# A factorization layer in a bilinear seven-product scheme: the first group begins with P1, and its sums T1 and T2 are made by VectorE

## The chip, the cores and the metric

The kernel runs on one core of a Trainium2 chip. The metric is device time in microseconds of one execution. The kernel before takes 1285.91 us, the median of three runs (1285.85 to 1286.28). Lower is better.

## What is computed

For a batch `x` (1024 x 512), a weight tensor (64 x 512 x 512), and a linear layer:

```python
out_lin = x @ lin_w.T + lin_b
xv = einsum('bf,efm->bem', x, weight)
zp = einsum('bf,efm->bem', square(x), square(weight))
interaction = 0.5 * sum(square(xv) - zp, axis=1)
return out_lin + interaction
```

The sum of `zp` over e is one product of `square(x)` with the weights' squares summed over e, so nearly all of the work is `xv`: a product of 1024 x 512 with 512 x 32768, of which each element is squared and added up over e.

## The kernel before

**Tiles and stages.** `xv` is made in 32 groups of 1024 columns each (loop over `h` at L773). In a group the product is split into 2 x 2 quadrants on each side: `x` into A11, A12, A21, A22 and the group's weights into w11, w12, w21, w22. Instead of eight products of quadrants there are seven, P1 to P7, of sums of quadrants (`OPERAND` names the sum on the side of x, `RHS` the weights'): P1 = A11 x w11, P2 = A12 x w21, P3 = R3 x w22, P4 = A22 x T4, P5 = R5 x T1, P6 = R6 x T2, P7 = R7 x (w12 + w22); signs stand on the side of x. T1 is the sum of the quadrants 0 and 1 (w11, w12), T2 is T1 plus quadrant 3 (w22), T4 is T2 plus quadrant 2 (w21); they are successive states of one tile T. The sums on the side of x (R5, R6, R7, R3) are made once.

**Three passes or plain.** A product of fp32 numbers is made of fast fp32r matmuls in three passes: both sides are split into pieces H, L and K, and H x H, L x L and K x K are added up with weights. A split (`split`, L627) of a weight tile takes ScalarE two passes (L, then H), GpSimd or VectorE one for L (by `SPLIT`, and by `FIRST` in group 0), and GpSimd one for K. In group 0 the products in `PLAIN` (P1 and P2) take the quadrants as they are, with plain fp32 matmuls: eight of 128 x 128 x 512, each recorded as two. A product in three passes has 24 short ones. Every product has two halves, each in a bank pair of PSUM (four pairs in turn), and the K pass of a product comes `LAG` half-halves after its H and L passes, behind the front of the next product. Between the two passes the bank is scaled or added to by VectorE (L366) or ScalarE.

**What goes from product to product.** P1's banks are copied to two tiles `p1`, P5's to tiles `p5` (L741, ScalarE); P6 adds p1 and p5 and keeps the sum in tiles `w`; P2, P3, P7 and P4 add p1 or w, and their results are squared by ScalarE (`sq`) and reduced by VectorE (`acc`). The squares of the weights (`wsq`) are made by ScalarE and reduced by VectorE for `zp`.

**Order of the products.** Within a group `ORDER` is P1, P6, P2, P3, P7, P5, P4, where the P5 is that of the next group. Group 0's own P5 stands ahead of the loop (L772).

**Before group 0** the linear layer is computed with the same scheme one level deep, in plain fp32 (L504, seven products of sixteen records each), while the quadrants of x are loaded and split (`x_pieces`, L482). Its four results lie in tiles that group 0 uses later: L12 in `p5_0`, L22 in `p1_0`, L21 in `p1_1`, L11 in `wsq_0`. They are added up by VectorE and stored to a buffer in DRAM (`lind`) by SP; only after the store may the tile be used again.

**Loads.** SP loads quadrants of weights (L606). The sums T and P7's operand are made by DMAs that add to a tile as they land (`dma_add` in `load_more`, L611), issued by GpSimd. The L and K pieces of A12 and A22 (`X2L`, `X2K`, `X4L`, `X4K`) are also made by such accumulate DMAs.

**What sets the order.** Nothing of it is written out by hand. Every operation is added to a list with its cost, reads and writes (`Plan.add`); a planner (`Plan.forward`) then gives every engine's queue its order by due times that follow from TensorE's fixed sequence, in 60 rounds with random changes of due times, and the best is kept. Each engine then runs its queue in order. A changed operation can therefore move others in the whole program. Operations of VectorE marked `both` read two tiles in SBUF; the planner puts them where GpSimd has no instruction that reads SBUF, or orders the two. In the first 70 us a DMA can be tied to the matmul that ended last before its planned start (`mark`).

**The tail.** After group 31 the products for `zp` are made like the linear layer; what `acc` holds is turned, stored to DRAM (`accd`), and added to the linear part in the tiles p1 and p5 by accumulate DMAs.

Of the kernel before, what the change touches and what calls it, by code (L numbers as in the profile page):

```python
# [22 lines left out]

PE, DVE, ACT, POOL, SP = "PE", "DVE", "ACT", "POOL", "SP"

PLAIN = (1, 2)
LAG = 4
ORDER = (1, 6, 2, 3, 7, 5, 4)
SPLIT = {**dict.fromkeys(range(1, 8), POOL), 2: DVE, 3: DVE}
MORE = True  # L30
X_SPLIT = {5: DVE, 6: DVE, 3: DVE, 7: DVE, 1: DVE, 2: "DMA", 4: "DMA"}
FIRST = dict.fromkeys(range(1, 8), POOL)
SCALE = {1: "DVE", 5: "ACT"}
RAW = {"w11": 2, "w12": 2, "w21": 1, "w22": 2, "T": 2}
PIECES = {"H": 3, "L": 3, "K": 3}
# [6 lines left out]
class Plan:  # L42
# [104 lines left out]
    def forward(self, chain):  # L147
# [4 lines left out]
        running = dict.fromkeys(pending)  # L152
        times = [self.HOP]
        done, late, nxt, wire, held, mark = [], 0.0, 0, [12.0], None, None
# [55 lines left out]
        while len(done) < len(ops):  # L210
            now = heapq.heappop(times)
            moved = True
            while moved:
                moved = False
                for e in pending:
                    if free[e] > now + 1e-6:
                        continue
                    o = pick(e, now)
                    if e == POOL and held is not None and (o is None or o.move):
                        ends(DVE, held, now + held.costs[DVE])  # L220
                        held = None
                    if o is None:
                        continue
                    moved = True
                    if e == PE:
                        nxt, mark = nxt + 1, running[PE]
                        late = max(late, now - o.latest)
                    cost = o.costs[e]
                    o.start, o.engine = now, e
                    if o.move and o.emit and mark and now < self.EARLY[0] and now > max(  # L230
                        ready(o, e) + 0.3, free[e] + 0.1
                    ):
                        o.after = mark
                    tensor = e == POOL and not o.move
                    if e == DVE and o.both and free[POOL] > now + 0.05 and not running[POOL].move:
                        held, free[e], o.end = o, float("inf"), float("inf")
                    elif tensor and held is not None and held.latest < o.latest + self.YIELD:
                        ends(DVE, held, now + held.costs[DVE])
                        o.after, held = held, None
                        ends(e, o, free[DVE] + 0.15 + cost)  # L240
                    elif tensor and held is None and free[DVE] > now and running[DVE].both:
                        o.after = running[DVE]
                        ends(e, o, free[DVE] + cost)
                    else:
                        ends(e, o, now + cost)
                    for f in o.costs:
                        pending[f].discard(o.n)
                    done.append((o, e))
                    for x in o.succ:
                        left[x] -= 1  # L250
                        if not left[x]:
                            release(ops[x])
# [4 lines left out]
def kernel(  # L257
# [47 lines left out]
    buf = {}  # L305
# [21 lines left out]
    raw = {q: ring(q, n, block) for q, n in RAW.items()}  # L327
# [42 lines left out]
    def dve(o, a, b, sub, reads, writes, size=512, both=False):  # L370
        def emit(_):
            return (nc.vector.tensor_sub if sub else nc.vector.tensor_add)(o, a, b)  # L372

        plan.add({DVE: 0.06 + 1.08 * size / 1024}, emit, reads, writes, both=both)

    def pool(o, a, b, sub, reads, writes, size=1024):
        def emit(_):
            return (nc.gpsimd.tensor_sub if sub else nc.gpsimd.tensor_add)(o, a, b)  # L378

        plan.add({POOL: 0.1 + 2.24 * size / 1024}, emit, reads, writes)  # L380
# [14 lines left out]
    def dma_add(o, i, reads, writes, move=3.1, land=2.5):  # L395
        plan.add(
            {POOL: 0.62}, lambda _: nc.gpsimd.dma_start(o, i, accum_op=ALU.add),  # L397
            tuple(reads) + tuple(writes), writes, land=land, move=move,
        )
# [200 lines left out]
    QUAD = ("w11", "w12", "w21", "w22")  # L600
    RHS = {1: "w11", 2: "w21", 3: "w22", 4: "T", 5: "T", 6: "T", 7: "w12"}
    now = {}

    def src(h, q):
        return weight[h // NCB, q][:, h % NCB]

    def load(h, n, q):
        now[h, n] = raw[n]()
        dma(buf[now[h, n]], src(h, q), (), (now[h, n],))

    def load_more(h, n, q):  # L611

        o = now[h, n]
        if h or MORE:
            dma_add(buf[o], src(h, q), (), (o,))
        else:
            i = now[h, QUAD[q]]
            pool(buf[o], buf[o], buf[i], False, (o, i), (o,))

    def w_squares(h, q):  # L620
        row, col = divmod(QUAD.index(q), 2)
        n, sq = now[h, q], wsquare()
        act(buf[sq], buf[n], AF.Square, (n,), (sq,))
        m = (h // NCB) * MG + (2 * col + h % NCB) * MI
        reduce(w2_sum[:, ts(row, KH), m:m + MI], buf[sq], (sq,), (("w2", row, m),))
# [16 lines left out]

    def prepare(h, p):
        if p == 5:
            load(h, "T", 0)
            if h:
                load_more(h, "T", 1)
                load(h, "w11", 0)
            load(h, "w12", 1)
            if not h:  # L650
                load_more(h, "T", 1)
                load(h, "w11", 0)
                load(h, "w22", 3)
                load(h, "w21", 2)
            w_squares(h, "w12")
        if p == 1:
            if h:
                load(h, "w22", 3)
            w_squares(h, "w11")
        if p == 6:  # L660
            load_more(h, "T", 3)
            if h:
                load(h, "w21", 2)
            w_squares(h, "w22")
        if p == 2:
            w_squares(h, "w21")
        if p == 7:
            load_more(h, "w12", 3)
        if p == 4:
            load_more(h, "T", 2)  # L670
        n = now[h, RHS[p]]
        return n if not h and p in PLAIN else split(n, SPLIT[p] if h else FIRST[p])

# [15 lines left out]
    def product(h, p):  # L689
        ops, plain = prepare(h, p), not h and p in PLAIN  # L690
        for half in range(2):
# [77 lines left out]

    for g in range(NG):  # L770
        acc_name[g] = acc_ring()
    product(0, 5)  # L772
    for h in range(NH):  # L773
        for p in ORDER:
            if p != 5:
                product(h, p)
            elif h + 1 < NH:
                product(h + 1, p)
            if not h:
                give_back(*(n for n in ("A11", "A12", "A22") if OPERAND[p] == n))  # L780
        if h % NCB == NCB - 1 and h + 1 < NH:
            turn(h // NCB)
# [64 lines left out]
    for (r, c), n in (((0, 0), "p1"), ((1, 0), "p1"), ((1, 1), "p5"), ((0, 1), "p5")):  # L847
        n = o_name[r, c] = kept[n]()
# [45 lines left out]
    for r in (1, 0):  # L894
        dma(buf[last][:, r], acc_dram[:, M // P - 1, ts(r, H)], acc_names(M // P - 1),
            ((last, r),), 1.0)
        n = o_name[r, 1]
# [56 lines left out]
```

## Time and profile before

| | |
|---|---|
| median of three runs | 1285.91 us |
| lowest, highest | 1285.85, 1286.28 us |
| the profiled execution | 1285.96 us, of which 1284.0 from the first instruction to the last |
| granted TensorE clock | 0.999 of full speed |
| moved by DMA | 171.93 MB, 134 GB/s over the span |

Instructions are named by engine: PE is TensorE's matmul and PEld its weight load, DVE is VectorE, ACT ScalarE, POOL GpSimd, SP SyncE. A row of a timeline has the start in us from the span's start, the duration, the engine, the line, the operation, what is written from what (numbers of buffers left out), the size, how many follow each other, and in brackets the idle time ahead of it with what ended it. Matmuls are pipelined and their ends are modelled, so the durations of neighbours overlap; times between starts are safer. In rows of DMAs stand the size of each and the median time from issue to landing. Names of pieces and tiles are cut in some rows: the tiles of the weights' quadrants and the kept tiles `w` both read `w`.

### The profile page before, as it was taken

How to read it: one execution, taken by the hardware profiler on the slowest of the kernel's cores; microseconds unless marked ns; L12 is line 12 of the kernel's file. 1: busy time of each engine (PE TensorE's matmuls, PEld its weight loads, DVE VectorE, ACT ScalarE, POOL GpSimd, SP SyncE). 2: the span in 40 equal slices, each digit the busy share in tenths (PEclk: the TensorE clock that was granted, in tenths of full speed). 3: DMA queues.
4: the chain of work that ended last, by engine and by line, in shares of the span. 5: the costliest groups of instructions: out<-in, count | busy, mean ns of one | idle time of the engine just before them, and what ended most of it. 6: DMA issues, size and time to landing. Idle time of an engine off the chain costs nothing.

```text
span 1284.0 us, 15422 instructions
## 1 busy us (share of the span) xinstructions
PE 1277.9 (100%) x5476; PEld 1024.1 (80%) x5476; DVE 1224.3 (95%) x1018; ACT 963.9 (75%) x1005; POOL 1043.5 (81%) x532
## 2 busy tenths in 40 slices
PE   9999999999999999999999999999999999999998
PEld 4688888888888888888888888888888888888883
DVE  7799999999999999999999999999999999999996
ACT  6677877777787777877777878777778777787781
POOL 2888898888898888898888888888889878889881
PEclk9999999999999999999999999999999999999999
DMA  8966654446654445664445664444665435665456
GB/s 237 210 175 148 148 118 123 101 108 151 148 129 123 99 110 139 152 142 118 108 102 130 148 152 115 120 98 114 152 148 128 120 85 122 145 152 131 126 112 168
DMA packets 68077, 171.93 MB, mean 134 GB/s; under 512 B 22944, under 2 KB 23968, under 8 KB 68000
## 3 DMA queue, kind: packets, MB, share of 16 engines
q0 software_dynamic: 20448, 72.89, 33.4%
q1 hardware_dynamic: 45296, 94.91, 22.1%
q10 hardware_dynamic: 2256, 3.15, 0.7%
q8 instruction: 43, 0.70, 0.2%
q14 instruction: 34, 0.28, 0.1%
HBM read 160.43 MB, written 6.29 MB: 130 GB/s over the span
## 4 chain that ended last, share of the span: by engine, by line
PE 94%; DVE 3%; DMA 2%; ACT 0%; issue 0%; ACTq 0%; SPq 0%; DVEq 0%
PE bank L697 92%; PE bank L522 2%; DMA w<-weight 1%; DMA p<-lin_wT 1%; DVE pL L366 0%; DVE bank L366 0%; DVE acc L385 0%; DVE X3K L366 0%; DVE p L372 0%; DVE w L372 0%; ACT pH L360 0%; ACT sq L360 0%; ACTq L427 0%; DVE X7K L366 0%; DVE sq L366 0%
## 5 line engine op out<-in xcount | busy, mean ns | idle before, releaser
L378 POOL TENSOR_TENSOR pK<-pH,pL 128x1024 fp32r<-128x1024 f32 x222 | 570.8, 2574 | 161.9 <-PE bank L697 157.5
L360 ACT ACTIVATE sq<-bank 128x1024 f32<-128x1024 f32 x256 | 261.9, 1024 | 93.8 <-issue 48.5
L385 DVE TENSOR_REDUCE acc<-sq 128x16 f32<-128x1024 f32 x256 | 308.5, 1205 | 1.3 <-ACT sq L360 1.2
L378 POOL TENSOR_TENSOR pL<-T,pL 128x1024 fp32r<-128x1024 f32 x96 | 256.7, 2674 | 12.9 <-ACT pH L360 10.7
L366 DVE SCALAR_TENSOR_TENSOR bank<-bank,w 128x1024 f32<-128x1024 f32 x192 | 233.8, 1218 | 0.7 <-PE bank L697 0.6
L372 DVE TENSOR_TENSOR w<-bank,p 128x1024 f32<-128x1024 f32 x128 | 155.6, 1216 | 26.8 <-PE bank L697 26.7
L360 ACT ACTIVATE p<-bank 128x1024 f32<-128x1024 f32 x128 | 131.0, 1023 | 59.9 <-PE bank L697 59.4
L366 DVE SCALAR_TENSOR_TENSOR pL<-pH,w 128x1024 fp32r<-128x1024 f32 x62 | 167.4, 2700 | 0.0
L366 DVE SCALAR_TENSOR_TENSOR bank<-bank,p 128x1024 f32<-128x1024 f32 x128 | 153.0, 1216 | 5.4 <-ACT p L360 4.5
L360 ACT ACTIVATE pL<-T 128x1024 fp32r<-128x1024 f32 x96 | 101.1, 1054 | 75.5 <-issue 68.3
L385 DVE TENSOR_REDUCE w_sum<-wsq 128x16 f32<-128x1024 f32 x128 | 154.1, 1204 | 2.5 <-ACT wsq L360 2.5
L378 POOL TENSOR_TENSOR pL<-w,pL 128x1024 fp32r<-128x1024 f32 x64 | 154.4, 2412 | 0.4 <-issue 0.4
L360 ACT ACTIVATE pH<-w 128x1024 fp32r<-128x1024 f32 x126 | 133.0, 1056 | 11.9 <-PE bank L697 10.3
L360 ACT ACTIVATE wsq<-w 128x1024 f32<-128x1024 f32 x128 | 134.6, 1052 | 0.4 <-DVE w_sum L385 0.4
L397 POOL DMA_DIRECT2D T<-weight x96 | 92.5, 963 | 36.7 <-POOL pL L378 17.5
L360 ACT ACTIVATE pH<-T 128x1024 fp32r<-128x1024 f32 x96 | 101.2, 1054 | 0.0
L360 ACT ACTIVATE pL<-w 128x1024 fp32r<-128x1024 f32 x64 | 67.9, 1061 | 43.6 <-PE bank L697 25.0
L697 PE MATMUL bank<-pH,X4H 128*128 128x512 f32 x256 | 81.4, 399 | 0.0
L697 PE MATMUL bank<-pH,X6H 128*128 128x512 f32 x256 | 78.9, 389 | 0.3 <-ACT p L360 0.3
L697 PE MATMUL bank<-pH,X5H 128*128 128x512 f32 x256 | 79.2, 391 | 0.0
L697 PE MATMUL bank<-pL,X4L 128*128 128x512 f32 x256 | 79.1, 390 | 0.0
L697 PE MATMUL bank<-pH,X3H 128*128 128x512 f32 x256 | 78.9, 390 | 0.1
(114 smaller groups left out, 2545.8 us busy)
## 6 DMA issues: line engine op xcount, KB each, us to landing
w<-weight SPq DMA_DIRECT2D x128, 512.0 KB, 5.8
T<-weight POOLq DMA_DIRECT2D x96, 512.0 KB, 6.1
T<-weight SPq DMA_DIRECT2D x32, 512.0 KB, 4.8
w<-weight POOLq DMA_DIRECT2D x32, 512.0 KB, 6.8
accd<-turned SPq DMA_DIRECT2D x64, 32.0 KB, 5.8
p<-lind SPq DMA_DIRECT2D x4, 512.0 KB, 4.5
out<-p ACTq DMA_DIRECT2D x8, 256.0 KB, 2.5
w<-xT SPq DMA_DIRECT2D x6, 256.0 KB, 4.9
```

Of the source, the lines that this page charges most:

```text
L360: nc.scalar.activation(o, i, func, bias=bias, scale=scale)
L366: return nc.vector.scalar_tensor_tensor(o, i, scalar, j, ALU.mult, op)
L372: return (nc.vector.tensor_sub if sub else nc.vector.tensor_add)(o, a, b)
L378: return (nc.gpsimd.tensor_sub if sub else nc.gpsimd.tensor_add)(o, a, b)
L385: lambda _: nc.vector.tensor_reduce(o, i.rearrange("p a (m e) -> p a m e", e=E), axis=AX.X, op=ALU.add),
L397: {POOL: 0.62}, lambda _: nc.gpsimd.dma_start(o, i, accum_op=ALU.add),
L522: made = nc.tensor.matmul(buf[bank[u]], b[:, k, ts(u, P)], a[:, k, :], start=first and k == 0, stop=k == KH - 1, skip_group_check=True,)
L697: made = nc.tensor.matmul(buf[bank, j], buf[x][:, k, ts(2 * half + j, P)], buf[w][:, k, :], start=first and k == 0, stop=k == KH - 1, skip ...
```

## The change

Group 0 is reordered and its operands are made in another way; the later groups' operations are the same.

- P1 of group 0 comes first, then its P5, then P6, P2, P3, P7, the next group's P5, and P4. Before, its P5 came first and P1 second.
- All four quadrants of group 0 are loaded as they are, w11, w12, w22, w21. T1 = w11 + w12 and T2 = T1 + w22 are VectorE additions into two tiles of the ring T (`sum_of`), instead of a load and two accumulate DMAs into one. T4 is still an accumulate DMA, into T2's tile.
- T1's L piece is made by VectorE (`FIRST`), not GpSimd.
- P2 of group 0 is made in three passes, and so w21 is split, and A12's pieces are needed there.
- The planner's `mark` skips an entry that has no instruction, and `MORE`, which was always true, is gone.

```diff
-PLAIN = (1, 2)
+PLAIN = (1,)
-MORE = True
-FIRST = dict.fromkeys(range(1, 8), POOL)
+FIRST = {**dict.fromkeys(range(1, 8), POOL), 5: DVE}
...
-                        nxt, mark = nxt + 1, running[PE]
+                        nxt += 1
+                        if running[PE] and running[PE].emit:
+                            mark = running[PE]
...
         o = now[h, n]
-        if h or MORE:
-            dma_add(buf[o], src(h, q), (), (o,))
-        else:
-            i = now[h, QUAD[q]]
-            pool(buf[o], buf[o], buf[i], False, (o, i), (o,))
+        dma_add(buf[o], src(h, q), (), (o,))
+
+    def sum_of(n, a, b):
+
+        o, a, b = raw[n](), now[0, a], now[0, b]
+        now[0, n] = o
+        dve(buf[o], buf[a], buf[b], False, (a, b), (o,), 1024, True)
...
         if p == 5:
-            load(h, "T", 0)
             if h:
+                load(h, "T", 0)
                 load_more(h, "T", 1)
                 load(h, "w11", 0)
-            load(h, "w12", 1)
-            if not h:
-                load_more(h, "T", 1)
-                load(h, "w11", 0)
-                load(h, "w22", 3)
-                load(h, "w21", 2)
+                load(h, "w12", 1)
+            else:
+                sum_of("T", "w11", "w12")
             w_squares(h, "w12")
         if p == 1:
             if h:
                 load(h, "w22", 3)
+            else:
+                for q in (0, 1, 3, 2):
+                    load(h, QUAD[q], q)
             w_squares(h, "w11")
         if p == 6:
-            load_more(h, "T", 3)
             if h:
+                load_more(h, "T", 3)
                 load(h, "w21", 2)
+            else:
+                sum_of("T", "T", "w22")
             w_squares(h, "w22")
...
-    product(0, 5)
     for h in range(NH):
         for p in ORDER:
             if p != 5:
                 product(h, p)
             elif h + 1 < NH:
                 product(h + 1, p)
+            if not h and p == 1:
+                product(h, 5)
```

How it moves instructions. In the names below the first number is the buffer in its ring: `w11_0` is quadrant w11 of group 0, while `w11_1` and `w12_1` hold A11 and A12 at this time.

TensorE, the first products behind the linear part, before:

```order
L522 MATMUL bank_3_117<-w_0_109,p5_2_113 128x512 x4
L697 MATMUL bank_0_114<-pH_0_95,X5H_77 128x512 x2
L697 MATMUL bank_0_114<-pL_0_98,X5L_78 128x512 x2
...
L697 MATMUL bank_2_116<-w11_0_86,w11_1_87 128x512 x4
L697 MATMUL bank_0_114<-pK_0_101,X5K_79 128x512 x4
L697 MATMUL bank_3_117<-w11_0_86,w11_1_87 128x512 x4
L697 MATMUL bank_1_115<-pK_0_101,X5K_79 128x512 x4
L697 MATMUL bank_0_114<-pH_1_96,X6H_80 128x512 x2
```

and now:

```order
L523 MATMUL bank_3_117<-w_0_109,p5_2_113 128x512 x4
L702 MATMUL bank_0_114<-w11_0_86,w11_1_87 128x512 x4
L702 MATMUL bank_1_115<-w11_0_86,w11_1_87 128x512 x4
L702 MATMUL bank_2_116<-pH_0_95,X5H_77 128x512 x2
L702 MATMUL bank_2_116<-pL_0_98,X5L_78 128x512 x2
...
L702 MATMUL bank_0_114<-pH_1_96,X6H_80 128x512 x2
L702 MATMUL bank_0_114<-pL_1_99,X6L_81 128x512 x2
```

Plain P1 (w11 with A11) now follows the linear part at once, and P6 takes the banks that P1 had, not those of P5.

VectorE at the end of the linear part, before:

```order
L372 TENSOR_TENSOR X6L_81<-sq_1_105,X6H_80 128x1024
L372 TENSOR_TENSOR X7L_84<-w_0_109,X7H_83 128x1024
L366 TENSOR_SCALAR X6K_82<-X6H_80,X6L_81 128x1024
L372 TENSOR_TENSOR X3L_72<-w_1_110,X3H_71 128x1024
L372 TENSOR_TENSOR p5_0_111<-p5_0_111,bank_2_116 128x512
L366 TENSOR_SCALAR X3K_73<-X3H_71,X3L_72 128x1024
L372 TENSOR_TENSOR p5_0_111<-p5_0_111,bank_2_116 128x512
L372 TENSOR_TENSOR p1_0_107<-p1_0_107,bank_3_117 128x512
L366 TENSOR_SCALAR X7K_85<-X7H_83,X7L_84 128x1024
```

and now:

```order
L373 TENSOR_TENSOR T_0_93<-w11_0_86,w12_0_88 128x1024
L373 TENSOR_TENSOR X5L_78<-sq_0_104,X5H_77 128x1024
L373 TENSOR_TENSOR T_1_94<-T_0_93,w22_0_91 128x1024
L367 TENSOR_SCALAR pL_0_98<-pH_0_95,T_0_93 128x1024
L373 TENSOR_TENSOR X6L_81<-sq_1_105,X6H_80 128x1024
L367 TENSOR_SCALAR X5K_79<-X5H_77,X5L_78 128x1024
L373 TENSOR_TENSOR p1_0_107<-p1_0_107,bank_3_117 128x512
...
L373 TENSOR_TENSOR p1_1_108<-p1_1_108,bank_3_117 128x512
L367 TENSOR_SCALAR X6K_82<-X6H_80,X6L_81 128x1024
L373 TENSOR_TENSOR X7L_84<-w_0_109,X7H_83 128x1024
L373 TENSOR_TENSOR X3L_72<-w_1_110,X3H_71 128x1024
L367 TENSOR_SCALAR X7K_85<-X7H_83,X7L_84 128x1024
```

T1, T2 and T1's L stand among the first pieces of x; X6K, X7L, X3L, X7K (and X3K, two rows on) stand behind the sums of the linear part in p1 and p5, of which the first reads the last linear product.

ScalarE, from group 0's first squares of weights on, now:

```order
L361 ACTIVATE wsq_0_106<-w12_0_88 128x1024
L361 ACTIVATE p1_0_107<-bank_0_114 128x1024
L361 ACTIVATE bank_2_116<-bank_2_116 128x1024
L361 ACTIVATE bank_3_117<-bank_3_117 128x1024
L361 ACTIVATE p1_1_108<-bank_1_115 128x1024
L361 ACTIVATE pL_0_98<-w22_0_91 128x1024
L361 ACTIVATE p5_0_111<-bank_2_116 128x1024
```

The copies of P1's banks to p1 now stand around the scaling of P5's banks; before, they came after the copies of P5's banks to p5 and after the splits for P6 and P3.

## The prediction

> **What bounds the kernel now.** First the busy shares and the list of who waited for whom on TensorE (engine, what it was to write, releaser; total us, times, longest).
>
> ```profile
> span 1284.0 us, 15422 instructions
> PE 1277.9 (100%) x5476; PEld 1024.1 (80%) x5476; DVE 1224.3 (95%) x1018; ACT 963.9 (75%) x1005; POOL 1043.5 (81%) x532
> PE bank L539 <- PEq L943: 0.8, 1, 0.8
> PE bank L522 <- issue: 0.6, 1, 0.6
> PE bank L697 <- ACT p L360: 0.3, 1, 0.3
> ```
>
> TensorE is the bound almost everywhere, and it waits three times in all. Time can therefore come only from fewer TensorE microseconds, or from the 0.3 and the 0.6. Next, busy time by stretch (length, then PE, PEld, DVE, ACT, POOL): group 0, then group 1.
>
> ```profile
> 29.23:69.06 39.83, 39.50 (x145) 26.85 (x144) 28.49 (x26) 26.30 (x28) 35.89 (x21) 1.00 0.90 209
> 69.06:107.20 38.14, 38.14 (x169) 31.37 (x169) 37.16 (x30) 29.98 (x32) 32.55 (x17) 1.00 0.66 174
> ```
>
> Group 1 fills TensorE without a gap at full clock, and so do all later ones, since no wait is left for them; group 0 takes 1.69 us longer. The TensorE timeline (start, duration) says where:
>
> ```profile
> 32.86 3.59 PE L697 MATMUL bank<-w,w 128*128 128x512 f32 x8
> ...
> 41.57 0.62 PE L697 MATMUL bank<-pH,X6H 128*128 128x512 f32 x2
> ...
> 43.87 0.73 PE L697 MATMUL bank<-pH,X6H 128*128 128x512 f32 x2 [0.33 <-ACT p L360]
> ...
> 45.82 3.59 PE L697 MATMUL bank<-w,w 128*128 128x512 f32 x8
> 48.85 1.48 PE L697 MATMUL bank<-pK,X6K 128*128 128x512 f32 x4
> 50.17 3.60 PE L697 MATMUL bank<-w,w 128*128 128x512 f32 x8
> 53.20 1.48 PE L697 MATMUL bank<-pK,X6K 128*128 128x512 f32 x4
> 54.53 0.62 PE L697 MATMUL bank<-pH,X3H 128*128 128x512 f32 x2
> ...
> 63.62 0.62 PE L697 MATMUL bank<-pH,X5H 128*128 128x512 f32 x2
> ...
> 69.06 0.62 PE L697 MATMUL bank<-pH,X4H 128*128 128x512 f32 x2
> ```
>
> Durations overlap, so I use starts. One product of 24 short matmuls takes 69.06 - 63.62 = 5.44 us, 0.227 each, so a block of four K matmuls takes 0.91.
>
> **The change, part by part.** *P2 in three passes.* Plain P2 is the two w,w rows at 45.82 and 50.17: 54.53 - 45.82 = 8.71, less two K blocks of 0.91, is 6.89 us. In three passes it is 5.44. TensorE saves **1.45 us**, all on the path.
>
> *The wait at 43.87.* From 41.57 to 45.82 stand sixteen short matmuls: 4.25 us where 16 x 0.227 = 3.63 belong. The gap marked 0.33 thus costs **0.62**. ScalarE was late with a copy, because its queue there held splits that followed accumulate DMAs and a store:
>
> ```profile
> 28.95 0.89 POOL L397 DMA_DIRECT2D T<-weight  x1 [0.31 <-POOL pL L378]
> 32.16 0.97 POOL L397 DMA_DIRECT2D w<-weight  x1
> 35.85 0.86 POOL L397 DMA_DIRECT2D T<-weight  x1
> 44.22 1.03 ACT L360 ACTIVATE p<-bank 128x1024 f32<-128x1024 f32 x1 [0.41 <-DMA lind<-p]
> ```
>
> With P1 first, P6 follows P5, and both T are sums of quadrants on chip. The copies that free P6's banks are then P1's (p1), which wait for P1 itself and for stores of the linear part out of the same p1 tiles. What is late next is therefore a store, not a split. I take the 0.62 as gone.
>
> *The T sums.* Group 0's two accumulate DMAs into T go, and one load. VectorE gets two additions and one L, GpSimd loses one subtraction (2.35), ScalarE one pass (1.06). The rows of SP, ScalarE and GpSimd, then VectorE's:
>
> ```profile
> 9.61 0.33 SPq L392 DMA_DIRECT2D T<-weight  x1
> T<-weight SPq DMA_DIRECT2D x1, 512.0 KB, 4.7
> 24.25 1.06 ACT L360 ACTIVATE pL<-T 128x1024 fp32r<-128x1024 f32 x1
> 26.29 2.35 POOL L378 TENSOR_TENSOR pL<-T,pL 128x1024 fp32r<-128x1024 f32 x1 [10.70 <-ACT pH L360]
> ...
> 17.52 1.22 DVE L366 SCALAR_TENSOR_TENSOR w<-sq,w 128x1024 f32<-128x1024 f32 x1
> 18.65 1.22 DVE L372 TENSOR_TENSOR X5L<-sq,X5H 128x1024 fp32r<-128x1024 f32 x1
> ...
> 26.66 3.06 DVE L366 SCALAR_TENSOR_TENSOR X3K<-X3H,X3L 128x1024 fp32r<-128x1024 f32 x1
> 29.65 1.27 DVE L372 TENSOR_TENSOR p<-p,bank 128x512 f32<-128x512 f32 x2
> ...
> 37.70 1.22 DVE L385 TENSOR_REDUCE w_sum<-wsq 128x16 f32<-128x1024 f32 x1 [1.39 <-ACT wsq L360]
> 40.04 1.22 DVE L385 TENSOR_REDUCE w_sum<-wsq 128x16 f32<-128x1024 f32 x1 [1.13 <-ACT wsq L360]
> 45.29 1.23 DVE L366 SCALAR_TENSOR_TENSOR bank<-bank,p 128x1024 f32<-128x1024 f32 x1 [4.02 <-ACT p L360]
> ```
>
> From start to start a full VectorE instruction takes 1.13 (18.65 - 17.52). From 17.52 I lay the new queue out: w, a half add of 0.6, T1 at 19.3, X5L, T2 at 21.5, L at 22.7, X6L, X5K to 26.1. Next stands a sum of the linear part that cannot start before the linear part ends: 32.86 - 16 x 0.227 = 29.2. So the 3.4 us added lie ahead of a wait of 3 us, and before GpSimd's first subtraction (26.29). T1 needs w11 and w12; their loads take the places of T's (9.61) and the one behind it, and by its 4.7 land before 16, X2L's accumulate beside them included. P5's H and L are there by 24, and P1 covers TensorE from 29.2 to 36.1: hidden, by 12 us. But X6K, X7L, X3L, X7K, X3K now stand behind the linear sums. VectorE had 1.39 + 1.13 + 4.02 = 6.5 us free there; five pieces of 1.14, plus waits for GpSimd like the one in X3K (3.06 - 1.22 = 1.84), eat it. X3K, the last of the five, waits for a subtraction of w22 that GpSimd starts at 42.9 to 43.6 (ScalarE's scaling of P5's second bank, ready at 39.7, the copy of p1_1 below and w22's pL come first, 1.06 each or less): 2.4 and 1.13 later, X3K ends at 46.4 to 47.1. Seventeen instructions on, 19.3 us without a pause, the sum is done that frees P4's first bank, at 65.7 to 66.4, and ScalarE's square (as long as the copy above, 1.03) at 66.8 to 67.5. TensorE wants P4 at 29.2 + 6.9 + 6 x 5.44 - 8 x 0.227 = 66.9 (the K matmuls of the product ahead come later). Bounds 0 and 0.8 (0.6 and a refill as at 43.87); I take **+0.3**.
>
> The Trainium skill, SBUF — State Buffer, section "SBUF: two separate sides", calls the port that VectorE with two SBUF inputs and GpSimd share an exclusive lock, held for the whole instruction by whichever starts first. X3K's 3.06 agrees. By it all turns on X5K at 24.9: first, and this term is 0; behind GpSimd, and it is 0.8.
>
> *Stores against P1's copies.* The stores of the linear part:
>
> ```profile
> 30.35 7.43 SPq L392 DMA_DIRECT2D lind<-p  x3
> DMA to landing us min/median/max: 4.3/7.4/10.2
> w<-weight POOLq DMA_DIRECT2D x1, 512.0 KB, 8.7
> X2L<-w POOLq DMA_DIRECT2D x1, 512.0 KB, 8.4
> X2K<-X2L POOLq DMA_DIRECT2D x1, 512.0 KB, 10.0
> ```
>
> Half of the four stores took over 7.4 us, one 10.2, with three accumulates (28.95 to 35.85) in flight. Afterwards p1_0's store leaves at 31.3 to 32.7 (29.4 plus three sums of 0.6, or 1.4 later behind GpSimd), p1_1's at 34.1 to 35.7. P6's two halves are due at 36.1 + 16 x 0.227 = 39.7 and at 42.5, and each copy takes 1.03, so the stores have 5.8 to 7.2 us. X2L and X2K, moved from about 52 and 62 to about 12 and 20, have landed by 30.5 by these rows; GpSimd's next accumulates stand behind five subtractions, at 37 or later. The stores travel nearly alone, nearer the row of 4.3: **0**. Upper bound in the rivals. SP's loads for group 1 queue behind these stores as before; their first use is after 66.
>
> *P2's split.* ScalarE 2 x 1.06, GpSimd 2 x 2.4, at about 27 to 39; P2 is due at 45.2. X2L and X2K land by 30.5. Hidden; without that cover GpSimd's 4.8 would show.
>
> *Everything later.* The order was drawn up anew, so each later group changes a little: GpSimd issues the accumulate into w12 two subtractions earlier, one into T later. T is read some 20 us after its issue, and these groups have no gap: 0; upper bound in the rivals.
>
> *The tail.* The 0.6 is here:
>
> ```profile
> 1270.39 0.69 DVE L372 TENSOR_TENSOR p<-p,w 128x512 f32<-128x512 f32 x1 [2.13 <-DMA p<-accd]
> 1272.57 3.67 PE L522 MATMUL bank<-T,T 128*128 128x512 f32 x8 [0.59 <-issue]
> p<-lind SPq DMA_DIRECT2D x1, 512.0 KB, 11.8
> ```
>
> A sum waits for an accumulate that waited for a load of 11.8 us. The new order issues one block of accd stores earlier and two p1 accumulates later; the load keeps its place. Bounds -0.7 (gone) and +1.0 (half of the 2.13 again); I take 0.
>
> **Sum** against the profiled execution: span 1284.0 - 1.45 - 0.62 + 0.3 = 1282.2; 1285.96 - 1284.0 = 1.96 lies around it, so 1284.2. That execution is 0.05 above the median, 1285.91; I say **1284.2**, 0.13% less.
>
> **Rivals.** *Stores as slow as before* (the slower side): X2K, or group 1's first load of T at 25.6, still fills the DMA engines. p1_0's store lands 10.2 after 32.7, at 42.9; the copy ends at 43.9; P6 starts 4.2 late. The scaling of P5's banks and the copy of p1_1 queue behind it on ScalarE: 0.5 more. 1284.2 - 0.3 + 4.7 = **1288.6**. It decides once the store takes over 5.8 us, and costs more than the change brings from 8 us on. For: the 10.2. Against: no accumulate at that hour.
>
> The Trainium skill, DMA: Bandwidth & Descriptors, section "SWDGE vs HWDGE vs iDMA", says each DMA engine takes turns between the queues that GpSimd's and the other engines' DMAs feed. One accumulate beside the store would then double the store's 4.3 to 8.6, making it 1287; 10.2 with three of them agrees.
>
> *VectorE becomes group 0's bound*: one or two more of the five pieces lose 1.84 to GpSimd, 1.84 to 3.7 that nothing behind them absorbs; in the middle 2.5 more, **1286.7**. Against: VectorE is 72% busy there (28.49 of 39.83).
>
> *The new order leaks* 0.1 us in each of 31 groups: +3.1, **1287.3**. For: VectorE has 38.14 - 37.16 = 1 us free per group. Against: it had no more before, and no gap came of it.
>
> *The tail wait goes too, and the VectorE term is 0*: 1284.2 - 0.3 - 0.7 = **1283.2**.
>
> **How the numbers follow.** Forecast 0.55 (its own range 1283.4 to 1285.4), tail 0.17, VectorE 0.11, leak 0.09, stores 0.08. 0.2% is 2.6 us, about what a measurement of this kernel can tell from no change: faster is below 1283.3, slower above 1288.5. Faster takes most of the tail case: 0.13. Slower takes the store case and a little of the leak: 0.11. Within: 0.76. The range reaches to the tail case and the leak, 1282.8 to 1287.4, and leaves out the stores.
>
> **What would show it.** Right: P2 as 24 short matmuls in 5.44; P1 from 29.2 without a pause to P5; no wait of TensorE on a p copy; T1 and T2 on VectorE before 24; P3 to P4 without a gap. Wrong: a wait of P6 on ACT p, released by a store (rival one); waits at P3 or P4 released by DVE (rival two); a group after 70 longer than 38.14 (leak). A start of P1 later than 29.4, because ScalarE's split of T1 stands ahead of the copies that the last linear product needs, would upset the whole layout.

## The result, and the profile after

Over 21 executions the changed kernel takes 1284.1 us (median; 1282.83 to 1286.65), the kernel before, in as many beside it, 1285.91 (1284.55 to 1289.82). The ratio is 0.9985, 95% interval 0.9978 to 0.9991: 0.15% faster. That is less than the 0.2% that the prediction takes as the limit of what can be told, but the interval lies wholly below 1. 1284.2 was predicted.

The profiled execution is one of the quickest of the 21: 1282.88 us, with 2.28 around its span. First the head of its page, and TensorE's list of waits (total, times, longest):

```profile
span 1280.6 us, 15506 instructions
PE 1275.7 (100%) x5484; PEld 1025.9 (80%) x5484; DVE 1230.9 (96%) x1021; ACT 962.1 (75%) x1006; POOL 1044.7 (82%) x531
PE bank L540 <- PEq L949: 0.8, 1, 0.8
```

Of the three waits of before only the one at the program's start is left. VectorE has gone from 95 to 96%. Next TensorE's timeline (start, duration) where the linear part ends and P1 begins, from a later profile of the same kernel (after_third, span 1280.5):

```profile
22.01 7.03 PE L523 MATMUL bank<-w,p 128*128 128x512 f32 x16
28.87 7.03 PE L702 MATMUL bank<-w,w 128*128 128x512 f32 x16
35.34 1.02 PE L702 MATMUL bank<-pH,X5H 128*128 128x512 f32 x2
```

P1 follows the linear part (22.01 + 6.87 = 28.88) and P5 follows P1 without a pause. In the first profile that end lies at 28.85, and P2, P4 and P1 of group 1 read:

```profile
44.79 0.61 PE L702 MATMUL bank<-pH,X2H 128*128 128x512 f32 x2
...
50.23 0.61 PE L702 MATMUL bank<-pH,X3H 128*128 128x512 f32 x2
...
65.64 1.07 PE L702 MATMUL bank<-pK,X7K 128*128 128x512 f32 x4
66.84 0.74 PE L702 MATMUL bank<-pH,X4H 128*128 128x512 f32 x2
...
72.49 0.61 PE L702 MATMUL bank<-pH,X1H 128*128 128x512 f32 x2
```

P2 takes 50.23 - 44.79 = 5.44, as 24 short matmuls. Behind the last K block before P4, P4 should start at 65.64 + 0.91 = 66.55; it starts at 66.84. That gap of 0.29 carries no bracket, but the two engines ahead of it show it, VectorE's sum and ScalarE's square:

```profile
64.46 1.20 DVE L373 TENSOR_TENSOR w<-bank,p 128x1024 f32<-128x1024 f32 x1
65.75 1.03 ACT L361 ACTIVATE sq<-bank 128x1024 f32<-128x1024 f32 x1 [0.50 <-DVE w L373]
```

The square waits for the sum, ends at 66.78, and P4 follows at 66.84. VectorE is busy without a pause before it, as the busy time by stretch shows (length, then PE, PEld, DVE, ACT, POOL with their instructions, granted clock, DMA share, GB/s), from the linear part's end to P4:

```profile
28.85:66.84 37.99, 37.86 (x154) 28.37 (x152) 37.80 (x32) 25.77 (x28) 35.47 (x20) 1.00 0.71 175
```

VectorE: 37.80 of 37.99. Before it was 28.49 of 39.83.

**Where the time went.** I cut every profile at the same four matmuls: the linear part's end (start of its last row of sixteen plus 6.87), P1 of group 1, the tail's first row, the tail's last row. All stretches are differences of such starts; two more profiles of the changed kernel and one of the kernel before are included (they are among the experiments). For the first profile of the kernel before this gives 22.32 + 6.87 = 29.19. The prediction counted back from 32.86 to 29.23, and the expectations below therefore have 45.36 for its G, where 45.40 stands here.

| stretch, us | before | again | changed | again | third |
|---|---|---|---|---|---|
| to the linear part's end | 29.19 | 29.58 | 28.85 | 30.27 | 28.88 |
| G: from there to P1 of group 1 | 45.40 | 45.64 | 43.64 | 43.69 | 43.58 |
| groups 1 to 31 | 1178.21 | 1178.34 | 1178.04 | 1178.00 | 1178.04 |
| tail, first to last row | 23.28 | 23.38 | 22.46 | 22.45 | 22.45 |
| last row to the end | 7.92 | 7.96 | 7.61 | 7.59 | 7.55 |
| span | 1284.0 | 1284.9 | 1280.6 | 1282.0 | 1280.5 |

Four of the five stretches repeat to 0.1 to 0.3 us within a kernel. By them the changed kernel gains 1.88 in G, 0.25 in the groups, 0.88 in the tail and 0.36 at the end, 3.4 in all. The first stretch, which the change does not touch on TensorE, varies by 1.4 between executions of one kernel. The median gain is smaller than 3.4: over all executions the changed kernel's span has a median of 1281.9 (21) and 1282.3 (11 more), the kernel before of 1283.9 to 1284.4 (27, 35 and 23), so some 2 us; and 2.2 lie around its span against 2.0 before.

### The profile page after: what moved, and what is told of

Read it like the earlier page. It is cut to its first block, busy times and chain, and to the rows that moved or that the text cites. A ratio compares the mean times of both kernels' runs of the same rounds, so it can differ in the third digit from the quotient of the medians.

```text
span 1280.6 us, 15506 instructions
## 1 busy us (share of the span) xinstructions
PE 1275.7 (100%) x5484; PEld 1025.9 (80%) x5484; DVE 1230.9 (96%) x1021; ACT 962.1 (75%) x1006; POOL 1044.7 (82%) x531
## 3 DMA queue, kind: packets, MB, share of 16 engines
q1 hardware_dynamic: 45152, 94.39, 25.7%
## 4 chain that ended last, share of the span: by engine, by line
PE 98%; DVE 1%; issue 0%; ACT 0%; ACTq 0%
PE bank L702 94%; PE bank L523 3%; PE bank L512 1%; DVE bank L367 0%; DVE acc L386 0%; PE bank L540 0%; DVE w_sum L386 0%; DVE w L373 0%; ACT sq L361 0%; DVE p L373 0%; ACTq L361 0%
## 5 line engine op out<-in xcount | busy, mean ns | idle before, releaser
L379 POOL TENSOR_TENSOR pK<-pH,pL 128x1024 fp32r<-128x1024 f32 x223 | 586.6, 2631 | 177.5 <-PE bank L702 169.4
L379 POOL TENSOR_TENSOR pL<-T,pL 128x1024 fp32r<-128x1024 f32 x95 | 237.9, 2504 | 1.0 <-ACT pL L361 1.0
L379 POOL TENSOR_TENSOR pL<-w,pL 128x1024 fp32r<-128x1024 f32 x65 | 175.1, 2694 | 0.0
L398 POOL DMA_DIRECT2D T<-weight x94 | 83.2, 978 | 9.2 <-POOL pL L379 9.0
L702 PE MATMUL bank<-pL,X5L 128*128 128x512 f32 x256 | 78.8, 389 | 0.0
L702 PE MATMUL bank<-pL,X6L 128*128 128x512 f32 x256 | 78.8, 389 | 0.0
## 6 DMA issues: line engine op xcount, KB each, us to landing
w<-weight POOLq DMA_DIRECT2D x32, 512.0 KB, 10.3
```

The costliest lines, as they stand in the source:

```text
L702: made = nc.tensor.matmul(buf[bank, j], buf[x][:, k, ts(2 * half + j, P)], buf[w][:, k, :], start=first and k == 0, stop=k == KH - 1, skip ...
```

## The experiments

G of each is cut in the same way as above. Ratios are to the kernel before, in executions on the same chip.

### p2_plain: the change with P2 plain

```diff
-PLAIN = (1,)
+PLAIN = (1, 2)
```

> The change, but P2 of group 0 plain again (two full-precision rows of eight matmuls). Measure: the stretch G from the end of the linear part to the first matmul of P1 of group 1, 45.36 us before and 43.64 after. Theory (three passes save 1.45 of TensorE, and VectorE's backlog gives 0.3 to 0.4 of it back at P4): P2 takes 6.9 again, TensorE wants P4 1.45 later, the backlog at P4 is hidden and its wait goes, so G is 44.7 (+1.05 to +1.15) and the time about 1.1 over the changed kernel's 1284.1. Rival (VectorE, busy without a pause from 40 on, sets the end of group 0 whatever TensorE does): G stays at 43.6 to 43.8. Rival (the new order alone brought the gain): G 43.6 too, with a wait of TensorE gone nowhere else.

Measured: 1287.24 us, ratio 1.0007 (0.9999 to 1.0016); G is 46.19, which none of the theories gave. The price of P2 and the missing wait at P4 are as expected: P4 starts right behind the K block, 69.30 + 0.91 = 70.21. What was not expected is a new wait of TensorE in P6, and ScalarE's queue ahead of it:

```profile
41.40 0.73 PE L702 MATMUL bank<-pH,X6H 128*128 128x512 f32 x2 [1.16 <-ACT p L361]
```

```profile
38.46 1.01 ACT L361 ACTIVATE bank<-bank 128x1024 f32<-128x1024 f32 x1 [9.34 <-PE bank L702]
39.38 1.05 ACT L361 ACTIVATE wsq<-w 128x1024 f32<-128x1024 f32 x1
40.33 1.01 ACT L361 ACTIVATE p<-bank 128x1024 f32<-128x1024 f32 x1
```

The copy of P1's bank (40.33) has no idle time of its own. It stands in the queue behind the scaling of P5's bank, and for that ScalarE idled 9.34 us, while P1's bank had been full since 33. The order was drawn up anew, and came out worse at this place.

### p2_plain_copy: the same, with the copy ahead of the scaling

```diff
+                    first = () if h else (value["p1", 0, half],)
-                    act(o, o, AF.Copy, names, names, scale=1 + U)
+                    act(o, o, AF.Copy, (*names, *first), names, scale=1 + U)
```

> P2 plain as in p2_plain, but ScalarE's copy of each bank of P1 is tied ahead of the scaling of P5's bank of the same half. In p2_plain the copy stood behind that scaling, ScalarE idled 9 us before it, and P6 waited 1.3. Theory (that wait came of the redrawn order on ScalarE, not of P2): the wait of P6 is gone, P2 plain costs 1.45, the wait at P4 stays away: G, the stretch from the end of the linear part to P1 of group 1, is 43.64 + 1.45 - 0.36 = 44.7, against 46.2 in p2_plain. Rival (P1's copy waits for the store of the linear part whatever stands ahead of it): P6 waits 1 or more still, G 45.7 or more.

Measured: 1285.68 us, ratio 0.9998 (0.9989 to 1.0006); G is 44.67, no wait in P6.

```profile
37.92 1.01 ACT L361 ACTIVATE p<-bank 128x1024 f32<-128x1024 f32 x1
39.66 1.01 ACT L361 ACTIVATE bank<-bank 128x1024 f32<-128x1024 f32 x1 [0.73 <-PE bank L702]
```

The copy waits for no store at 37.92, in time for P6 at 41.27. So the wait in p2_plain was an order of ScalarE's queue. And P2 plain costs 44.67 - 43.64 = 1.03: 1.45 on TensorE less what VectorE's backlog no longer adds, as the sum had it.

### p2_alone: the kernel before with P2 in three passes

```diff
-PLAIN = (1, 2)
+PLAIN = (1,)
```

> The kernel before, P5 first and T by accumulate DMAs, with P2 of group 0 in three passes and nothing else. Theory (the two gains add up and do not need each other): P2 takes 5.44, the wait of P6 on ScalarE's copy stays at 0.62, VectorE has 6.5 us free so that no wait comes at P4: G = 45.36 - 1.45 = 43.9, time 1284.5. Rival (the room for P2's split and for X2L and X2K had to be made by taking T's accumulates away): the copy that frees P6's bank, or X2K, comes later than before, TensorE waits 1.5 or more in group 0, G 45.4 to 47.

Measured: 1287.37 us, ratio 1.0009 (1.0000 to 1.0017); G is 45.73. The rival's outcome, by another wait than it named. TensorE, then GpSimd:

```profile
31.67 0.73 PE L697 MATMUL bank<-pL,X5L 128*128 128x512 f32 x2 [2.18 <-POOL pL L378]
```

```profile
25.96 2.36 POOL L378 TENSOR_TENSOR pL<-w,pL 128x1024 fp32r<-128x1024 f32 x1 [7.08 <-DVE X3L L372]
28.29 3.33 POOL L378 TENSOR_TENSOR pL<-T,pL 128x1024 fp32r<-128x1024 f32 x1
```

GpSimd takes P2's new split (the first row, L of w21) ahead of T1's L, for which P5, the first product here, waits 2.18. The 1.45 of P2 and the 0.62 of the old wait, which does not appear, are gained and given back: 45.40 - 1.45 - 0.62 + 2.36 (the gap in starts, 31.67 - 28.86 - 0.45) = 45.69.

### order_alone: P1 first and P2 in three passes, T by accumulate DMAs

```diff
-                sum_of("T", "w11", "w12")
+                load(h, "T", 0)
+                load_more(h, "T", 1)
...
-                sum_of("T", "T", "w22")
+                load_more(h, "T", 3)
```

> The changed kernel with P1 first and P2 in three passes, but T of group 0 loaded and added by accumulate DMAs as before. Theory: VectorE's 3.4 us (two sums and one L) lie ahead of a pause of 3.3 us and cost nothing, so without them VectorE gains nothing at P4; what changes is that P5 and P6 wait for accumulates that run beside the linear part's stores. T1 is due 6.9 us later than before, so P5 is in time; the copies of P1 behind the stores or T2's split come late: TensorE waits 0.3 to 1.0 in P6, G 43.9 to 44.6. Rival (stores and accumulates share the DMA engines as in the prediction's first rival): P6 waits 3 to 5 us for ScalarE's copy, G 47 to 48. Rival (the sums on VectorE are what makes its backlog): the wait at P4 goes and nothing comes for it, G 43.3.

Measured: 1288.31 us, ratio 1.0019 (1.0010 to 1.0028); G is 47.99, the size that the rival of the stores gave. The views say who was late. ScalarE, then TensorE's rows behind the wait:

```profile
36.39 1.06 ACT L361 ACTIVATE wsq<-w 128x1024 f32<-128x1024 f32 x1 [2.47 <-DVE w_sum L386]
37.77 1.01 ACT L361 ACTIVATE bank<-bank 128x1024 f32<-128x1024 f32 x1 [0.31 <-PE bank L703]
38.74 1.06 ACT L361 ACTIVATE wsq<-w 128x1024 f32<-128x1024 f32 x1
39.71 1.04 ACT L361 ACTIVATE pL<-T 128x1024 fp32r<-128x1024 f32 x1
40.65 1.04 ACT L361 ACTIVATE pH<-T 128x1024 fp32r<-128x1024 f32 x1
41.60 1.00 ACT L361 ACTIVATE p<-bank 128x1024 f32<-128x1024 f32 x1
```

```profile
42.65 1.22 PE L703 MATMUL bank<-pH,X6H 128*128 128x512 f32 x2 [3.11 <-ACT p L361]
43.67 1.05 PE L703 MATMUL bank<-pL,X6L 128*128 128x512 f32 x2
```

P1's copy (41.60) stands behind the squares and T2's split. T2 is complete only after its second accumulate, which GpSimd issues at 29.66, while in the changed kernel its split is on ScalarE at 24.46. And the wait costs more than itself: the matmuls behind it are slow (below). 43.64 - 0.36 + 3.27 + 1.49 = 48.04. So with T by accumulates, P1 first brought a loss in this drawn order, and the sums on VectorE avoid it. That no order could do without them is not shown: the accumulate landed 5.9 after its issue, near 35.6, and ScalarE sat idle until 36.39, then took two squares and a scaling ahead of the split at 39.71. Nor is it shown that the sums cost VectorE nothing. It pauses for 3.29 behind them in the changed kernel (row of 29.04, below), but here, without them, it made X6K, X7L and X3L ahead of the linear part's sums in p, from 22.29 to 25.7, and in the changed kernel these three stand behind such sums.

### x7_dma: two VectorE pieces of group 0 by accumulate DMAs

```diff
-X_SPLIT = {5: DVE, 6: DVE, 3: DVE, 7: DVE, 1: DVE, 2: "DMA", 4: "DMA"}
+X_SPLIT = {5: DVE, 6: DVE, 3: DVE, 7: "DMA", 1: DVE, 2: "DMA", 4: "DMA"}
```

> The changed kernel with X7L and X7K made by ScalarE copies and accumulate DMAs in place of two VectorE instructions of 1.13 us in the middle of its backlog. Theory (the 0.29 at P4 is VectorE's backlog from the linear sums to the sum that frees P4's first bank): 2.3 us less backlog, the wait at P4 is gone, G = 43.64 - 0.3 to 0.4 = 43.3, time 0.3 less than the changed kernel's, unless the two accumulates are late. Rival (the gap at P4 comes from ScalarE's queue, which here gets one copy more): the gap stays or grows to 1, G 43.6 to 44.4. Rival (more accumulates slow the stores of the linear part): P6 waits for a copy, G over 45.

Measured: 1284.17 us, ratio 0.9980 (0.9971 to 0.9989); G is 43.29, 0.35 less than in the changed kernel, as the theory had it. TensorE at P4:

```profile
66.77 1.07 PE L702 MATMUL bank<-pK,X7K 128*128 128x512 f32 x4
67.68 0.63 PE L702 MATMUL bank<-pH,X4H 128*128 128x512 f32 x2
```

66.77 + 0.91 = 67.68: no gap. The wait at P4 was VectorE's backlog, and it cost 0.29 and a little refill.

### after_again, before_again, after_third: the same kernels once more

No edit.

> The changed kernel once more, instruction for instruction, for what differs between executions. If the tail is a matter of the drawn order, its eight last rows take 22.5 from first to last matmul row again, with no wait; if it is chance, 22.5 to 23.6. The linear part's end (28.85 in the first profile) and the stretch from the last row of matmuls to the end of the span (7.6) are expected to vary by 1 and by 2 us, since the loads at the start and the stores at the end have done so in the runs so far (28.9 to 29.9 and 7.6 to 9.7). G stays within 0.1 of 43.64.

> The kernel before once more, instruction for instruction. Drawn order: the wait of 0.6 in the tail is there again, 23.3 from its first to its last row of matmuls. Chance: 22.5. G within 0.1 of 45.36; the linear part's end and the last stores vary as in the changed kernel.

> The changed kernel a third time, instruction for instruction, timed beside the three above. G 43.6 to 43.7, tail 22.5 without a wait; the linear part's end anywhere from 28.7 to 30.8. Time 1284.1 within 0.7.

Measured: 1284.21 and 1286.94 us in one execution each; the third 1284.55, ratio 0.9985 (0.9976 to 0.9994). Their stretches stand in the table above. The tail's wait is there in both profiles of before (0.59, 0.69) and in none of the three of the changed kernel. The other redrawn orders have it or not: 0.90 in p2_plain, 0.29 in p2_plain_copy, 1.62 in rehome_x7, none in six. So it belongs to each drawn order, and the change did not aim at it. G of before_again, 45.64, is 0.24 over the first profile's 45.40, and that is its wait in P6, 0.57 in place of 0.33.

### p1_x7_act: P1 in three passes too

```diff
-PLAIN = (1,)
+PLAIN = ()
-X_SPLIT = {5: DVE, 6: DVE, 3: DVE, 7: DVE, 1: DVE, 2: "DMA", 4: "DMA"}
+X_SPLIT = {5: DVE, 6: DVE, 3: DVE, 7: "DMA", 1: DVE, 2: "DMA", 4: "DMA"}
...
-                elif SCALE[p] == ACT:
+                elif SCALE[p] == ACT or not h:
```

> The changed kernel with X7 by accumulate DMAs (as x7_dma, G 43.3) and P1 of group 0 in three passes too, ScalarE scaling its banks. Theory (TensorE bounds group 0 once VectorE has slack): P1 takes 5.44 in place of 6.87, G = 43.3 - 1.43 = 41.9 if VectorE's slack from x7_dma, some 2 us at P4, covers P4 being due 1.4 earlier; time 1282.7. Rival (P1's pieces or the copies behind the stores are late, being due 1.4 to 7 earlier): a wait of 1 to 4 at P1, P5 or P6, G 43 to 46, no gain.

Measured: 1290.38 us, ratio 1.0029 (1.0019 to 1.0039); G is 49.57, over the rival's upper end, and the groups behind take 1179.9, 1.9 more than in the changed kernel. The last 2.49 of G lie between the last K block before P1 of group 1 and P1 itself; without them it would be the 47.1 of the expectation below. The waits of TensorE:

```profile
PE bank L702 <- ACT p L361: 4.4, 2, 2.3
PE bank L702 <- DVE p L373: 0.9, 1, 0.9
```

One of the two waits for a copy is P6's (2.07 at 41.32), the other stands before P1 of group 1 (2.33 at 78.31). My expectation for rehome_x7_p1_act misread them as both in P6.

### rehome_x7 and rehome_x7_p1_act: P1's copies in tiles that nothing is stored from

```diff
-    "A21": "p1_0", "lt0": "p1_1", "lw1": "p5_1", "lt1": "p5_2",
+    "A21": "p5_1", "lt0": "p5_2", "lw1": "p1_0", "lt1": "p1_1",
```

> x7_dma, and four tiles of the linear part change places, so that P1's copies go into tiles from which nothing is stored (lw1 and lt1 lay in p5_1 and p5_2, and now lie in p1_0 and p1_1; A21 with L22 and lt0 with L21 go the other way). Theory (in the changed kernel the stores were hidden, VectorE alone gave the wait at P4): G, from the end of the linear part to P1 of group 1, is 43.3 as in x7_dma, and P1's copies stand right behind P1. Rival (the stores did cost something unseen): G under 43.1. Rival (the late stores now meet P5's copies): a wait in P6 or P2, G 44 or more.

Measured: 1284.17 us, ratio 0.9985 (0.9976 to 0.9994); G is 43.26, as in x7_dma. The stores did not show in the changed kernel. Its tail waits 1.62, drawn by lot.

> rehome_x7 with P1 of group 0 in three passes as well, its banks scaled by ScalarE: p1_x7_act without the stores in front of P1's copies. In p1_x7_act (G 47.1) P6 waited 2.1 and 2.3 for those copies and P5 0.9 for a sum of VectorE. Theory (the stores in the p1 tiles made those waits): the 4.4 go, P5's 0.9 may stay, G = 47.1 - 4.4 - 0.6 of slower refill = 42 to 42.8, less than rehome_x7. Rival (the copies were late because ScalarE's queue is full of splits and scalings, stores or not): waits of 2 or more in P6, G 44.5 to 47.

Measured: 1290.22 us, ratio 1.0035 (1.0022 to 1.0049). G is 43.54, between the theory's and the rival's: P6's wait is gone, P5 waits 0.46 for VectorE and P2 0.69 for a copy of P5. But the groups behind take 1185.2, 7 us more than in the changed kernel. TensorE and ScalarE at that place:

```profile
78.48 0.73 PE L702 MATMUL bank<-pH,X1H 128*128 128x512 f32 x2 [2.75 <-ACT p L361]
```

```profile
76.46 1.06 ACT L361 ACTIVATE pL<-T 128x1024 fp32r<-128x1024 f32 x1 [3.72 <-DMA T<-weight]
77.42 1.01 ACT L361 ACTIVATE p<-bank 128x1024 f32<-128x1024 f32 x1
```

ScalarE stands before a split of group 1's T that has not landed, with the copy behind it that P1 of group 1 waits for. It is like the stall at 43.87 of the kernel before, one group later, and p1_x7_act has it too, with a wait of 3.39 for T. The accumulate that this split waits for left GpSimd at 65.67 and took 10.7 to land; in x7_dma the like one left at 56.77 and took 7.1. Why GpSimd came to it so late was not tried. What P1 gave up in group 0 was lost again in waits there and in group 1.

### rehome_p1: more work for VectorE, less for TensorE

P1 in three passes with its banks scaled by VectorE, X7 on VectorE, tiles as in rehome_x7.

> P1 of group 0 in three passes, its banks scaled by VectorE (2 x 1.13 more there), X7 on VectorE as in the changed kernel, tiles changed as in rehome_x7. TensorE has 1.43 less to do than in the changed kernel, VectorE 2.3 more. Theory (in the changed kernel VectorE's backlog ends at P4 just as TensorE does, so VectorE now sets the end of group 0): the waits of TensorE at P3 to P4 grow to 3.5 to 4.5, G = 43.64 + 2.3 = 45.9, between 45 and 47. Rival (TensorE still bounds, VectorE has slack somewhere): G = 43.64 - 1.43 = 42.2 plus 1 at most.

Measured: 1284.34 us, ratio 0.9988 (0.9980 to 0.9997); G is 44.37, between the two. The waits are VectorE's, as the theory said, but earlier than P4 and smaller:

```profile
PE bank L702 <- DVE bank L739: 0.9, 1, 0.9
PE bank L702 <- DVE bank L367: 0.6, 1, 0.6
```

Between the linear part and 70 us VectorE makes one reduction of the weights' squares here, at 29.03, against five in the changed kernel. Four of 1.13 were put off, 4.5 in all against the 2.3 added. VectorE's backlog is real, but part of it can be moved.

## Why the prediction was right, and where it was not

**P2 in three passes, -1.45: right.** 6.89 to 5.44, and p2_plain_copy gives it back with 1.03 after VectorE's share.

**The wait at 43.87, -0.62: right that it goes.** The reason given, that what is late next is a store, was not borne out. In p2_plain and order_alone the late copy stood behind other work in ScalarE's own queue; with the copy moved ahead, no store held it. The prediction also misread a row. The copy that waited for a store, at 44.22, is the one behind the late one. The late one, in the kernel before, is the second row here:

```profile
40.90 1.06 ACT L360 ACTIVATE pL<-w 128x1024 fp32r<-128x1024 f32 x1 [0.89 <-DMA w<-weight]
...
42.81 1.01 ACT L360 ACTIVATE p<-bank 128x1024 f32<-128x1024 f32 x1
```

It stood behind the split of a tile w whose accumulate (issued at 32.16, for P7's operand) had just landed. So what was removed is a place in a queue behind an accumulate, not T's and not a store, and another order can make a like place anywhere.

**VectorE's backlog, +0.3: right in place, mechanism and size.** 0.29 in the trace, 0.35 by x7_dma. That the size fits so well is partly luck, since 0.3 was a pick between bounds of 0 and 0.8. The rows that the layout foretold, VectorE's and then GpSimd's:

```profile
21.12 1.22 DVE L373 TENSOR_TENSOR T<-T,w 128x1024 f32<-128x1024 f32 x1
...
24.53 1.22 DVE L367 SCALAR_TENSOR_TENSOR X5K<-X5H,X5L 128x1024 fp32r<-128x1024 f32 x1
29.04 3.08 DVE L373 TENSOR_TENSOR p<-p,bank 128x512 f32<-128x512 f32 x5 [3.29 <-PE bank L523]
...
33.76 2.27 DVE L367 SCALAR_TENSOR_TENSOR X6K<-X6H,X6L 128x1024 fp32r<-128x1024 f32 x1
...
37.09 3.42 DVE L373 TENSOR_TENSOR X3L<-w,X3H 128x1024 fp32r<-128x1024 f32 x1
...
42.70 3.76 DVE L367 SCALAR_TENSOR_TENSOR X3K<-X3H,X3L 128x1024 fp32r<-128x1024 f32 x1
```

```profile
24.76 3.21 POOL L379 TENSOR_TENSOR pK<-pH,pL 128x1024 fp32r<-128x1024 f32 x1 [2.88 <-DVE X6L L373]
```

The sums and the L were done by 23.4 and a pause of 3.29 stood behind them. X3K ended at 46.46, inside the 46.4 to 47.1 of the layout. Where it went astray is what hung on X5K: X5K went first (24.53 against 24.76), and the term was still 0.29, not 0, since three later pieces lost 1.05, 2.20 and 2.54 to GpSimd (their durations less 1.22), where the layout had one such loss. That two engines exclude each other there, as the Trainium skill has it (SBUF — State Buffer, section "SBUF: two separate sides"), agrees with these rows; it was wrong to let the term hang on one meeting.

**Stores, 0: right.** The stores' row in the DMA list of the changed kernel (size, median time to landing), and ScalarE's copy of P1's first bank, which stands behind a square and waits for no store:

```profile
lind<-p SPq DMA_DIRECT2D x3, 512.0 KB, 3.6
```

```profile
34.24 1.01 ACT L361 ACTIVATE p<-bank 128x1024 f32<-128x1024 f32 x1
```

The slowest took 4.5, where the prediction had room for 5.8 to 7.2. With an accumulate beside them, in order_alone, they took 5.7 in the median, and in p1_x7_act, with two, 8.6, the longest 10.3: what the first rival feared happens when accumulates are in flight, and here none were. Rehome_x7, where no store can hold these copies, has the same G.

**P2's split, hidden: right in the new order only.** In p2_alone 2.18 of GpSimd's share showed. Whether the cover is P1 in front or T1's L on VectorE, which takes it out of GpSimd's queue, was not tried apart.

**Groups 1 to 31, 0: right.** 1178.0 against 1178.2 to 1178.3.

**The tail, 0: wrong.** The step that failed is "the load keeps its place". The block of accd stores that the new order issues earlier had stood in front of that load on SP. Of the kernel before:

```profile
1248.91 4.66 SPq L392 DMA_DIRECT2D accd<-turned  x4
1253.67 2.12 SPq L392 DMA_DIRECT2D p<-lind  x1
```

Of the changed kernel, the same queue and the load's first and last issue:

```profile
1230.84 1.78 SPq L393 DMA_DIRECT2D accd<-turned  x4
1234.26 15.36 SPq L393 DMA_DIRECT2D p<-lind  x3
```

```profile
L393 SPq DMA_DIRECT2D p<-lind x4: 360/376/377, 1213.9 to 1249.3; - x4
```

The last load leaves at 1249.3, 1.2 before the tail's first row of matmuls (1250.53); in the kernel before it left at 1253.7, 0.9 behind that row (1252.80). The wait of 0.59 is gone, with refill 0.82, as in the fourth rival. In rehome_x7, where the load leaves 0.9 behind that row again, the wait is back, with 1.62. From the last row to the end it is 7.6 in the changed kernel and 7.9 in the kernel before, in every profile; other orders without a wait gave 7.6 to 9.7. Why was not tried.

**The sum.** Group 0 was right to 0.1 (-1.77 predicted, -1.76 measured, -1.88 over the repeats). The tail and the end gained 1.2 that the sum did not have, which would have put the time near 1283. That the median still is 1284.1, only 0.1 from the forecast, is luck: what the sum took from one execution and held constant came out longer by about as much. What lies around the span is 0.2 longer. And the first stretch is no constant: the profiled execution, with 28.85, is quick, while the one at 1284.21, next to the median, has the same kernel's stretches to 0.1 and a linear part that ends at 30.27. Over all fourteen profiles that end lies between 28.7 and 30.8. Whether the change itself lengthens the start can't be told from three profiles against two, and stays open. An estimate: the four later stretches add up to 1251.6 to 1251.8 in the changed kernel's profiles and to 1254.8 to 1255.3 in those of the kernel before. If they are as constant in the other executions, the median spans (1281.9 and 1282.3; 1283.9 to 1284.4) leave 30.1 to 30.7 for the start of the changed kernel and 28.6 to 29.6 for the other, about 1 us more. The loads of weights that the change issues early need not be the reason: rehome_x7 issues them as early, and the same working leaves 28.5 for it. The spread was under-read too: the first three times of before lay within 0.43, all 21 within 5.3.

No kernel here is clearly better than the changed one. x7_dma has 0.35 less in G, but its ratio's interval covers the changed kernel's.

## What to carry to other kernels

Where one engine is the bound and the others run in fixed queues, as here, a product made cheaper brings its full price only if its pieces cost no place in a queue that an earlier product waits in. P2 in three passes alone made G 0.3 longer, with the new order but T by accumulates 2.6 longer, and with the sums on VectorE as well 1.8 shorter. Each of these is one order drawn by the planner, and the differences hold for these orders. Read the gap behind the last K block against the short matmul's step: a wait of 0.29 has no bracket, and the rows ahead of it still name the engine that comes next as the bound (VectorE, in rehome_p1). When a planner redraws the whole order, take profiles of the same kernel twice and compare by stretches, since the tail's luck (0 to 1.6 us) and the start's (2 us) are as large as the change.

## What the runs showed that was not expected

A wait of TensorE over some 2 us can be followed by matmuls at half speed for a while. The busy time by stretch behind the waits (the granted clock, a mean over the stretch, is the third number from the end), first of p1_x7_act behind 2.07 and 2.33, then of order_alone behind 3.11, then of p2_alone behind 2.18:

```profile
41.32:46.00 4.68, 4.68 (x14) 3.68 (x14) 2.78 (x2) 2.75 (x3) 4.68 (x4) 0.64 0.67 221
78.31:84.00 5.69, 5.69 (x18) 4.53 (x19) 3.82 (x1) 4.72 (x5) 5.58 (x4) 0.70 0.94 176
```

```profile
42.65:46.86 4.21, 4.21 (x13) 3.37 (x14) 0.68 (x1) 3.70 (x4) 4.13 (x3) 0.65 1.00 242
```

```profile
31.67:36.00 4.33, 4.33 (x17) 3.27 (x18) 3.95 (x5) 1.83 (x2) 4.08 (x4) 1.00 0.77 152
```

In order_alone the twelve matmuls from 42.65 to 46.86 take 4.21 where 12 x 0.227 = 2.72 belong: 1.49 on top of the wait. Behind 2.18 the clock stayed at 1.00, behind 2.07 it fell.

The traces' record of the granted clock shows what the means hide. The clock is at 0.50 from 42.15 to 45.56 in order_alone, from 42.28 to 45.70 and from 79.83 to 83.25 in p1_x7_act, and from 79.47 to 82.89 in rehome_x7_p1_act (behind its 2.75), and at 1.00 outside these within the groups. Each slow stretch lasts 3.41 us, and in p1_x7_act the two begin 37.55 apart, which is eleven times 3.413: the clock seems to be set anew once per window of 3.41, wherever the wait lies. In the window ahead of each slow one TensorE sat idle for 2.6, 2.1, 1.9 and 2.4 us, by the waits' rows. The wait of 2.18 in p2_alone, if its windows are counted in the same way from where the clock first reads 1.00 (3.93), fell on two of them, 1.7 in the one and 0.4 in the next. Between 1.7 and 1.9 idle out of 3.41 would then be the limit, an estimate from five cases. The Trainium skill, TensorE: Matmul & The Clock Gate, section "Part 1: The HAM clock gate", has the clock halved after an idle window of about 3.4 us that runs freely, not from the wait's start. The window's length and its running freely agree with these traces; that waits of 2.07 to 3.11, all shorter than a window, were enough does not agree with a window that is idle throughout.
